# Delta rule into MLP on one core: another order in the last round, on SyncE's queue, and for the norm weight

## The chip, the core and the metric

The kernel runs on one core of a Trainium2 chip. The metric is the device time of one launch in microseconds (us), lower is better; the median of several runs is given with their lowest and highest.

## What is computed

The input x has 128 sequences of 32 tokens with 512 features (4096 tokens), the context 257 positions per sequence. Three residual steps follow each other; the change lies in the second.

```
x = x + cross_attention(layernorm(x), context)
x = x + delta_block(layernorm(x))
x = x + hadamard_quantised_ffn(layernorm(x))           # inner width 2048

delta_block(x):                                        # 32 heads of 16 features
    h = rms(x) * attn_norm
    q, k, v = silu(silu(causal_conv4(h @ W.T)))        # one W and one conv each
    q, k = q / |q|, k / |k| (per head);  beta = sigmoid(h @ Wbeta.T)
    per token, per head:  S -= beta * (S k - v) k^T;  o = S q
    x = x + (rms(o) * out_norm) @ Wout.T
    h2 = rms(x) * mlp_norm
    return x + (silu(h2 @ Wgate.T) * (h2 @ Wup.T)) @ Wdown.T      # inner width 1408
```

All of it is in fp32, apart from the last step's quantised matrices. The norm weights are not ones: they are drawn around one.

## The kernel before

Four stages follow each other: cross_attention, delta_products, delta_out_mlp, and hadamard_ffn, with a Substitution (the solution of the delta rule's triangular systems, on VectorE) that is run in slices beside the second and third. Between stages data goes through DRAM buffers: kd (normal k and q of the last group), ld and pd (products of k with k and of q with k), vd (v with beta), rq (one over the length of q), ud (solutions).

**delta_products** works in 8 rounds of 512 tokens (groups). A round has 12 steps, each the 128 output channels of one of q, k, v: `channels` runs four matmuls of 128x512 (L520), ScalarE scales the last tap (L525), VectorE adds three taps (L527), `activated` applies silu twice (L534, L535). Order of a round: k and q alternating for four chunks, then v four times. Beside the steps run the products of the group before (`multiply`, L455, from masked copies kqm that SyncE loads, L550), the sums of squares per head on TensorE (`Group.add`, L579 to L581), their square roots (`lengths`, L588), the transposition of lengths and beta to tokens (`by_tokens`, L594 to L604), the reciprocal of q's lengths and its store to rq (L606 to L609), and `put_v`: transposes of v (L618), scaling (L621), beta put beside it (L624, GpSimd), store to vd (L625). In each round put_v handles the v of the group before; in the last round there is no later round, so its own four put_v follow the last step. In the last round k and q are stored to kd by SyncE (L666) rather than masked at once, since the products of that group ("late products") are made in the next stage.

**delta_out_mlp** works in 16 blocks of 256 tokens, two tiles of 128 each. `back(b)` prepares block b: per tile it loads u (L743) and copies it to um (GpSimd, L750), loads pe in eight pieces (L757), multiplies (L764), loads xs (L771) and r (L773), and writes oT, the product of both (L777); then squares and a mean over features (L780 to L783), the matmul with Wout (L797), residual and norm (L800 to L811), and the transposition (L97) into hT, copied by ScalarE (L812). `mlp(b)` runs 11 steps of gate and up matmuls (L823, L826) with silu and product (L828, L829), then the down-projection (L834). `late_products` makes 16 products of the last group; each needs eight loads into the single buffer km (L856) and one of k (L858). `mixed` interleaves such generators by their costs: it always advances the one with the smallest share of its total done. Within a block mlp, back of the next block, two late products and the substitution are mixed.

The first block has no block before it. Ahead of it stand the loads of the weights (load_rows, L103: wo, then the norm weight mnw at L874, wg and wu in two halves of columns, the causal mask cm at L879), the first four units of `back(0)` and one late product, the loading of the out-norm weight onw and its multiplication onto wo (scaled_rows, L403 and L406, on VectorE), the load of wd, 16 multiplications of mnw onto wg and wu (L888, on ScalarE), and the rest of back(0) with three late products. The program is written as one sequence; a scheduler then sets each engine's own order, an engine runs its order strictly, and so does each engine's queue of DMA issues. SyncE issues nearly all loads, GpSimd most stores. A DMA issue on SyncE also waits for the transfer that it issued eight before. Tile pools hold buffers; a stage's pools lie where those of the stage before lay, so a first load into a tile waits for the last reader of what lay there.

Of the kernel before, what the change touches and what calls it, by code (L numbers as in the profile page):

```python
# [100 lines left out]
def load_rows(nc, dst, src):  # L101

    nc.sync.dma_start(dst, src.rearrange("(c p) n -> p c n", p=P))  # L103
# [361 lines left out]
def delta_products(  # L465
# [11 lines left out]
    stack, (xp, wp1, hp, wk1, wp, st, wk, wp2, wk2, wp3, wk3, psn, psp, ps, psg) = pools(  # L477
        tc, ("b_x", 3), ("b_w1", 1), ("b_hn", 2), ("b_h", 2), ("b_w", 1), ("b_st", 2), ("b_k", 2),
        ("b_w2", 1), ("b_v", 2), ("b_m", 4), ("b_g", 6), ("b_pn", 1, PSUM), ("b_pp", 3, PSUM),
        ("b_ps", 2, PSUM), ("b_pg", 2, PSUM),  # L480
    )
    with stack:
        w, cw = {}, {}
        for n, src, p in (("k", wkT, wp1), ("q", wqT, wp1), ("v", wvT, wp2)):
            w[n] = p.tile([P, DC, D], FP, name=f"w{n}")
            load_rows(nc, w[n], src)
# [11 lines left out]
        kqm = [wp3.tile([P, HH, 2, KT], FP, name=f"kqm{i}", bufs=1) for i in range(3)]  # L498
# [67 lines left out]
        class Group:  # L566
# [16 lines left out]
            def lengths(self):  # L583

                f = self.factors = wk.tile([3 * H, SG], FP, name="f", bufs=1)
                nc.scalar.activation(f[H : 2 * H], self.sums[H : 2 * H], AF.Tanh, scale=0.5)
                for r in (slice(0, H), slice(2 * H, 3 * H)):
                    nc.scalar.activation(f[r], self.sums[r], AF.Sqrt)  # L588

            def by_tokens(self):  # L590
# [13 lines left out]
                nc.vector.tensor_mul(self.beta, self.beta, n2)  # L604
                q = f[2 * H :]
# [32 lines left out]
        def a_round(gi, old, hT, made):  # L638
# [3 lines left out]
            if gi + 1 < NG:  # L642
                hT_next = wk1.tile([P, DC, SG], FP, name="hT")
                made.append(hT_next)
            for j, (n, ec) in enumerate(todo):
                if n == "v":
                    dst = new.v[ec] = wk2.tile([P, SG], FP, name="v2", bufs=4)
                else:
                    if n == "k":
                        kq[ec] = wp3.tile([P, 2, SG], FP, name="kq")  # L650
                    dst = kq[ec][:, "kq".index(n)]
# [9 lines left out]
                if n == "q":  # L661
                    if gi < NG - 1:
                        pieces.extend((gi, ec, half, kq[ec]) for half in range(SG // KT))
                        hold()
                    else:
                        nc.sync.dma_start(kd[:, ec], kq[ec])  # L666
                if 3 <= j <= 9 and j % 2:
                    new.add(kq[(j - 3) // 2], hT, (j - 3) // 2)
                if j in loads and gi + 1 < NG:
# [7 lines left out]
                if j >= 8 and gi + 1 < NG:  # L677
# [4 lines left out]
            if gi + 1 == NG:  # L682
                for ec in range(DC):
                    new.put_v(ec)

# [4 lines left out]
        for gi in range(NG):  # L690
            made = []
            mixed((len(todo), a_round(gi, old, hT, made)), *beside(gi))
            old, hT = made[0], made[-1]
# [3 lines left out]
def delta_out_mlp(  # L697
# [14 lines left out]
    with stack:  # L712
# [6 lines left out]
        cm = lp.tile([P, T], FP, name="cm")  # L719
        wo = wp.tile([P, DC, D], FP, name="wo")  # L720
        wg = wp.tile([P, DC, FF], FP, name="wg")
        wu = wp.tile([P, DC, FF], FP, name="wu")
        wd = wp.tile([P, FC, D], FP, name="wd")
# [9 lines left out]
        def back(b):  # L733
# [76 lines left out]
            for i in range(NTL):  # L810
                nc.vector.tensor_scalar_mul(ys[i], ys[i], r[:, i : i + 1])  # L811
                nc.scalar.copy(hT[:, :, i * P : (i + 1) * P], g.transposed(ps, ys[i], g.ident))  # L812
# [60 lines left out]
        nw = st.tile([P, DC], FP, name="mnw", bufs=1)  # L873
        nc.sync.dma_start(nw, norm_w.rearrange("(c p) -> p c", p=P))  # L874

        for cols in (slice(0, 6 * P), slice(6 * P, FF)):
            for t, src in ((wg, wgT), (wu, wuT)):
                load_rows(nc, t[:, :, cols], src[:, cols])
        nc.sync.dma_start(cm, causal)  # L879
        mark = []  # L880
        first, late = back(0), late_products()
        mixed((4.0, part(first, 4.0)), (1.0, part(late, 1.0)))
        scaled_rows(nc, st, "onw", onorm_w, [wo])
        load_rows(nc, wd, wdT)
        for cols in (slice(0, 6 * P), slice(6 * P, FF)):
            for t in (wg, wu):
                for dc in range(DC):
                    nc.scalar.mul(t[:, dc, cols], t[:, dc, cols], nw[:, dc : dc + 1])  # L888
        mixed((12.0, first), (3.0, part(late, 3.0)))
# [306 lines left out]
```

## Time and profile before

| | us |
|---|---|
| median of 3 runs | 3079.94 |
| lowest, highest | 3078.09, 3083.41 |
| the profiled execution | 3080.81 |
| its span | 3079.0 |
| TensorE (PE) busy | 2934.2 (95%) |
| VectorE (DVE) busy | 2059.5 (67%) |
| ScalarE (ACT) busy | 1090.1 (35%) |
| GpSimd (POOL) busy | 706.0 (23%) |

About 1.8 us of the execution lie around the span. The mean clock that TensorE was granted is 0.984 of full speed. A page of the profile shows busy time in 40 slices of 77 us, the costliest groups of instructions by line, and a chain of waits, followed back from the end; SPq, DVEq and so on are the engines' sequencers, an L number is a line of the kernel. Matmuls of fp32 appear as two records each, and records of one engine may overlap slightly.

The stages on the time axis: cross_attention to about 706 us, delta_products to 1229 us (its last round begins at 1176.20), first gate matmul of the MLP at 1288.49 us, last blocks done at about 2415 us, then the Hadamard FFN.

### The profile page before, as it was taken

Reading aid. Unit: us, or ns where it says so; the run is one execution under the profiler, and the core shown is the slowest. Engines: PE = TensorE matmul, PEld = TensorE weight load, DVE = VectorE, ACT = ScalarE, POOL = GpSimd, SP = SyncE. Lnnn points to the kernel's source line nnn. Section 1 sums busy time; section 2 is a strip of 40 time slices with the busy share of each in tenths; the row PEclk is TensorE's granted clock in tenths of the full one; section 3 lists DMA queues with packets and bytes.
Section 4 is the critical chain, followed back from the end, with each engine's and each line's share of the span. In section 5 each row is a group of like instructions: output and inputs, shape, how many; then the busy total and the mean of one; then the engine's idle time right before and its main releaser. Section 6 shows DMA issues by size and latency. Waiting matters only on the chain.

```text
span 3079.0 us, 42048 instructions
## 1 busy us (share of the span) xinstructions
PE 2934.2 (95%) x15558; PEld 1683.7 (55%) x15558; DVE 2059.5 (67%) x3432; ACT 1090.1 (35%) x1812; POOL 706.0 (23%) x995
## 2 busy tenths in 40 slices
PE   8999999999999999599999999999999899999997
PEld 3444344443333333367676666667777566666664
DVE  2353434326699797378778787878422599999996
ACT  1111111215656666312221112111111366666665
POOL 1121212112686675321212111011000010000001
PEclk9999999999999999799999999999999999999998
DMA  9797989863554544641423323131411111111110
GB/s 332 265 311 269 307 306 310 274 213 98 166 148 131 173 129 132 198 126 59 128 74 106 97 66 112 48 101 50 139 42 42 55 42 42 42 42 35 39 31 21
DMA packets 258236, 408.09 MB, mean 133 GB/s; under 512 B 68336, under 2 KB 170864, under 8 KB 254576
## 3 DMA queue, kind: packets, MB, share of 16 engines
q1 hardware_dynamic: 223856, 305.21, 31.7%
q0 software_dynamic: 34176, 100.19, 9.5%
q8 instruction: 124, 2.03, 0.3%
q14 instruction: 80, 0.66, 0.1%
HBM read 288.36 MB, written 93.85 MB: 124 GB/s over the span
## 4 chain that ended last, share of the span: by engine, by line
PE 41%; DVE 17%; ACT 5%; issue 3%; DMA 2%; SPq 0%; POOL 0%; DVEq 0%; POOLq 0%; ACTq 0%
PE pm L834 9%; PE pm L823 9%; PE pm L826 9%; PE pp L520 5%; PE ps L797 3%; DVE mb L127 3%; ACT t L956 3%; DVE mb L126 2%; DVE mx L1016 2%; DVE m L126 2%; PE pg L455 2%; PE ps L764 2%; DVE m L1002 1%; DVE m L127 1%; DVE W L442 1%
## 5 line engine op out<-in xcount | busy, mean ns | idle before, releaser
L823 PE MATMUL pm<-hT,wg 128*128 128x256 f32 x1408 | 342.1, 386 | 0.7 <-ACT hT L812 0.7
L826 PE MATMUL pm<-hT,wu 128*128 128x256 f32 x1408 | 333.3, 379 | 0.0
L436 DVE TENSOR_TENSOR pr<-L,W 128x1984 f32<-128x1984 f32 (+30 forms) x248 | 312.1, 1258 | 24.6 <-DMA L<-ld 20.6
L442 DVE TENSOR_TENSOR W<-W,pr 128x1984 f32<-128x1984 f32 (+30 forms) x248 | 309.0, 1246 | 3.2
L834 PE MATMUL pm<-wd,mT 128*128 128x512 f32 x704 | 307.2, 592 | 0.0
L823 PEld LDWEIGHTS pm<-hT,wg 128*128 128x128 f32 x1408 | 262.2, 191 | 57.5 <-issue 16.2
L826 PEld LDWEIGHTS pm<-hT,wu 128*128 128x128 f32 x1408 | 267.2, 190 | 36.2
L834 PEld LDWEIGHTS pm<-wd,mT 128*128 128x128 f32 x704 | 132.6, 190 | 160.8 <-issue 160.7
L828 ACT ACTIVATE sg<-pm 128x256 f32<-128x256 f32 x176 | 67.4, 383 | 350.1 <-PE pm L823 340.1
L829 DVE TENSOR_TENSOR mT<-pm,sg 128x256 f32<-128x256 f32 x176 | 73.8, 419 | 164.1 <-PE pm L826 150.0
L1042 POOL TENSOR_TENSOR xo<-xo,xt 128x512 f32<-128x512 f32 x32 | 42.7, 1336 | 581.6 <-ACT xo L1041 581.6
L996 PE MATMUL ps<-wq,qT 128*128 128x512 bf16 x512 | 133.1, 383 | 28.9 <-DVE m L1002 17.3
L956 ACT ACTIVATE t<-ps,magic,qs 128x512 f32<-128x512 f32 x160 | 117.6, 777 | 96.5 <-DVE qs L951 96.4
L461 POOL TENSOR_TENSOR kk<-kk,cm 128x256 f32<-128x256 f32 x128 | 135.5, 1058 | 2.1
L999 PE MATMUL ps<-wq,qT 128*128 128x512 bf16 x512 | 132.4, 381 | 2.2 <-DVE m L1002 2.2
L458 POOL DMA_DIRECT2D ld<-kk x128 | 92.2, 720 | 147.4 <-ACT kk L457 140.4
L346 PE MATMUL ps<-hT,wq 128*128 128x512 f32 x256 | 118.6, 623 | 7.2 <-ACT hT L339 7.2
L939 PE MATMUL ps<-hd,mT 128*128 128x128 f32 x1024 | 121.5, 277 | 0.0
L455 PE MATMUL pg<-kqm,kq 128*32 128x512 f32 x896 | 118.8, 601 | 2.1 <-DMA kqm<-kq 1.5
L302 PE MATMUL ps<-wo,aoT 128*128 128x512 f32 x256 | 118.8, 608 | 1.5 <-ACT aoT L295 1.5
L520 PE MATMUL pp<-hT,wk 128*128 128x512 f32 x256 | 118.6, 604 | 0.3 <-DVE acc L527 0.3
L1039 PE MATMUL ps<-wq,q2T 128*128 128x512 bf16 x512 | 117.2, 383 | 0.9 <-ACT q2T L1033 0.9
(217 smaller groups left out, 5220.6 us busy)
## 6 DMA issues: line engine op xcount, KB each, us to landing
kall<-in_ctxT_dram SPq DMA_DIRECT2D x32, 2056.0 KB
cx<-in_ctx_dram SPq DMA_DIRECT2D x32, 2048.0 KB
x<-xo POOLq DMA_DIRECT2D x64, 256.0 KB, 3.4
xt<-x SPq DMA_DIRECT2D x64, 256.0 KB
ld<-kk POOLq DMA_DIRECT2D x128, 128.0 KB, 2.5
pd<-kk POOLq DMA_DIRECT2D x128, 128.0 KB, 2.3
L<-ld SPq DMA_DIRECT2D x8, 2048.0 KB
pe<-pd SPq DMA_DIRECT2D x256, 64.0 KB
```

Source lines behind the costliest of these rows:

```text
L126: nc.vector.tensor_add(o[:, :, 0, :], i[:, :, 0, :], i[:, :, 1, :])
L436: nc.vector.tensor_mul(pr[:, 0:n], bc(L[:, s, :, s + 1 : T].rearrange("p h t -> p t h"), HD), w[:, s].unsqueeze(1).to_broadcast([P, n, H4, ...
L442: nc.vector.tensor_sub(w[:, s + 1 :], w[:, s + 1 :], pr[:, 0:n])
L455: nc.tensor.matmul(pg[js], k[:, js], m[:, :, :, js], start=True, stop=True)
L461: nc.gpsimd.tensor_mul(kk[:, 1], kk[:, 1], cm.unsqueeze(1).to_broadcast([P, HH, T]))
L520: nc.tensor.matmul(pp.rearrange("p b t -> p (b t)"), w[n][:, dc, ec * P : (ec + 1) * P], hT[:, dc, :], start=dc == 0, stop=dc == DC - 1,)
L823: nc.tensor.matmul(pg, wg[:, dc, fs], hT[:, dc, :], start=dc == 0, stop=dc == DC - 1)
L826: nc.tensor.matmul(pu, wu[:, dc, fs], hT[:, dc, :], start=dc == 0, stop=dc == DC - 1)
L834: nc.tensor.matmul(pd, mT[:, fc, i * P : (i + 1) * P], wd[:, fc, :], start=fc == 0, stop=fc == FC - 1,)
L956: nc.scalar.activation(t, pr, AF.Identity, bias=magic, scale=qs)
L996: nc.tensor.matmul(pg, qT[:, dc, :], wg[:, dc, ks], start=dc == 0, stop=dc == DC - 1)
L999: nc.tensor.matmul(pu, qT[:, dc, :], wu[:, dc, ks], start=dc == 0, stop=dc == DC - 1)
```

## The change

It has four parts.

1. In delta_products the weights wq and wv swap pools and the order of loading: wv is now loaded early with wk, wq where wv was. The pairs kq get a pool of their own, kqm too.
2. The last round is a function of its own, `last_round`: the order of its steps is k four times, v four times, q four times. Two products run per step. The sums of squares are made separately for k (with beta) and for q (`add_one`); lengths and by_tokens for k and beta come in the v steps; each q step stores its pair to kd from ScalarE's queue and puts one chunk of the group's own v away; q's lengths and their reciprocal (`put_q`, split off by_tokens) come last.
3. In delta_out_mlp SyncE's order changes: wo, wg, wu, wg, wu first, then all loads of back(0) for both tiles (four units of it), then cm, onw and mnw, then wd, then the late products' loads; all four of the early late products now come after the first four units of back(0). The tile of wd is allocated ahead of the other weights.
4. The MLP's norm weight is no longer multiplied onto wg and wu. Instead the transposed norm output is multiplied by it on its way into hT: per tile four pieces of 128x128, two on ScalarE and two on VectorE.

```diff
--- before.py
+++ after.py
@@ -100,7 +100,7 @@
 
 def load_rows(nc, dst, src):
 
-    nc.sync.dma_start(dst, src.rearrange("(c p) n -> p c n", p=P))
+    return nc.sync.dma_start(dst, src.rearrange("(c p) n -> p c n", p=P))
 
 
 def mixed(*steps):
@@ -474,14 +474,14 @@
     tc, nc = g.tc, g.nc
     KT = 256
 
-    stack, (xp, wp1, hp, wk1, wp, st, wk, wp2, wk2, wp3, wk3, psn, psp, ps, psg) = pools(
+    stack, (xp, wp1, hp, wk1, wp, st, wk, wp2, kqp, wk2, wp3, wk3, psn, psp, ps, psg) = pools(
         tc, ("b_x", 3), ("b_w1", 1), ("b_hn", 2), ("b_h", 2), ("b_w", 1), ("b_st", 2), ("b_k", 2),
-        ("b_w2", 1), ("b_v", 2), ("b_m", 4), ("b_g", 6), ("b_pn", 1, PSUM), ("b_pp", 3, PSUM),
+        ("b_w2", 1), ("b_kq", 4), ("b_v", 2), ("b_m", 1), ("b_g", 6), ("b_pn", 1, PSUM), ("b_pp", 3, PSUM),
         ("b_ps", 2, PSUM), ("b_pg", 2, PSUM),
     )
     with stack:
         w, cw = {}, {}
-        for n, src, p in (("k", wkT, wp1), ("q", wqT, wp1), ("v", wvT, wp2)):
+        for n, src, p in (("k", wkT, wp1), ("q", wqT, wp2), ("v", wvT, wp1)):
             w[n] = p.tile([P, DC, D], FP, name=f"w{n}")
             load_rows(nc, w[n], src)
         w["b"] = wp.tile([P, DC, H], FP, name="wb")
@@ -495,7 +495,7 @@
         nc.sync.dma_start(cm, causal)
         scaled_rows(nc, wp, "nw", norm_w, [w["k"], w["q"], w["v"], w["b"]])
 
-        kqm = [wp3.tile([P, HH, 2, KT], FP, name=f"kqm{i}", bufs=1) for i in range(3)]
+        kqm = [wp3.tile([P, HH, 2, KT], FP, name=f"kqm{i}") for i in range(3)]
         blank = [t[:, h] for t in kqm for h in range(HH)]
         mv, rs = stats
 
@@ -580,12 +580,24 @@
                 nc.tensor.matmul(self.sums[H : 2 * H], w["b"][:, ec, :], hT[:, ec, :], **at)
                 nc.tensor.matmul(self.sums[2 * H :], hs[:, ec, :], sq[:, 1], **at)
 
-            def lengths(self):
-
-                f = self.factors = wk.tile([3 * H, SG], FP, name="f", bufs=1)
-                nc.scalar.activation(f[H : 2 * H], self.sums[H : 2 * H], AF.Tanh, scale=0.5)
-                for r in (slice(0, H), slice(2 * H, 3 * H)):
-                    nc.scalar.activation(f[r], self.sums[r], AF.Sqrt)
+            def add_one(self, kq, hT, ec, of):
+
+                sq = wk.tile([P, 2, SG], FP, name="sq")
+                nc.scalar.activation(sq[:, 0], kq[:, "kq".index(of)], AF.Square)
+                at = dict(start=ec == 0, stop=ec == DC - 1)
+                rows = slice(0, H) if of == "k" else slice(2 * H, 3 * H)
+                nc.tensor.matmul(self.sums[rows], hs[:, ec, :], sq[:, 0], **at)
+                if of == "k":
+                    nc.tensor.matmul(self.sums[H : 2 * H], w["b"][:, ec, :], hT[:, ec, :], **at)
+
+            def lengths(self, of="kq"):
+
+                if "k" in of:
+                    f = self.factors = wk.tile([3 * H, SG], FP, name="f", bufs=1)
+                    nc.scalar.activation(f[H : 2 * H], self.sums[H : 2 * H], AF.Tanh, scale=0.5)
+                for n, r in (("k", slice(0, H)), ("q", slice(2 * H, 3 * H))):
+                    if n in of:
+                        nc.scalar.activation(self.factors[r], self.sums[r], AF.Sqrt)
 
             def by_tokens(self):
                 f = self.factors
@@ -602,6 +614,9 @@
                 nc.vector.tensor_mul(n2, self.n, self.n)
                 nc.vector.reciprocal(n2, n2)
                 nc.vector.tensor_mul(self.beta, self.beta, n2)
+
+            def put_q(self):
+                f = self.factors
                 q = f[2 * H :]
                 nc.vector.tensor_scalar_max(q, q, 1e-12)
                 nc.vector.reciprocal(q, q)
@@ -639,15 +654,14 @@
             new = Group(gi)
             made.append(new)
             xt, kq = [], {}
-            if gi + 1 < NG:
-                hT_next = wk1.tile([P, DC, SG], FP, name="hT")
-                made.append(hT_next)
+            hT_next = wk1.tile([P, DC, SG], FP, name="hT")
+            made.append(hT_next)
             for j, (n, ec) in enumerate(todo):
                 if n == "v":
                     dst = new.v[ec] = wk2.tile([P, SG], FP, name="v2", bufs=4)
                 else:
                     if n == "k":
-                        kq[ec] = wp3.tile([P, 2, SG], FP, name="kq")
+                        kq[ec] = kqp.tile([P, 2, SG], FP, name="kq")
                     dst = kq[ec][:, "kq".index(n)]
                 acc, last = channels(hT, n, ec)
                 with tc.issue_after(last):
@@ -659,14 +673,11 @@
                         multiply()
                 activated(acc, dst)
                 if n == "q":
-                    if gi < NG - 1:
-                        pieces.extend((gi, ec, half, kq[ec]) for half in range(SG // KT))
-                        hold()
-                    else:
-                        nc.sync.dma_start(kd[:, ec], kq[ec])
+                    pieces.extend((gi, ec, half, kq[ec]) for half in range(SG // KT))
+                    hold()
                 if 3 <= j <= 9 and j % 2:
                     new.add(kq[(j - 3) // 2], hT, (j - 3) // 2)
-                if j in loads and gi + 1 < NG:
+                if j in loads:
                     xt.append(load((gi + 1) * GT + len(xt)))
                 if j == 9:
                     new.lengths()
@@ -674,23 +685,57 @@
                         g.factors(*(t[:, EARLY:] for t in stats))
                 if j == 11:
                     new.by_tokens()
-                if j >= 8 and gi + 1 < NG:
+                    new.put_q()
+                if j >= 8:
                     normed((gi + 1) * GT + j - 8, xt[j - 8], hT_next)
                 if old and j < DC:
                     old.put_v(j)
                 yield 1
-            if gi + 1 == NG:
-                for ec in range(DC):
+
+        def last_round(gi, old, hT):
+
+
+            new = Group(gi)
+            kq = []
+            for j, (n, ec) in enumerate((n, ec) for n in "kvq" for ec in range(DC)):
+                if n == "k":
+                    kq.append(kqp.tile([P, 2, SG], FP, name="kq"))
+                if n == "v":
+                    dst = new.v[ec] = wk2.tile([P, SG], FP, name="v2", bufs=4)
+                else:
+                    dst = kq[ec][:, "kq".index(n)]
+                acc, _ = channels(hT, n, ec)
+                for _ in range(2):
+                    if count["done"] < per * len(held):
+                        multiply()
+                activated(acc, dst)
+                if n == "q":
+                    nc.scalar.dma_start(kd[:, ec], kq[ec])
                     new.put_v(ec)
+                if j < DC:
+                    old.put_v(j)
+                if 1 <= j <= DC:
+                    new.add_one(kq[j - 1], hT, j - 1, "k")
+                elif j == DC + 1:
+                    new.lengths("k")
+                elif j == DC + 2:
+                    new.by_tokens()
+                elif n == "q" and ec:
+                    new.add_one(kq[ec - 1], hT, ec - 1, "q")
+                yield 1
+            new.add_one(kq[DC - 1], hT, DC - 1, "q")
+            new.lengths("q")
+            new.put_q()
 
         hT = wk1.tile([P, DC, SG], FP, name="hT")
         for i in range(GT):
             normed(i, load(i), hT)
         old = None
-        for gi in range(NG):
+        for gi in range(NG - 1):
             made = []
             mixed((len(todo), a_round(gi, old, hT, made)), *beside(gi))
-            old, hT = made[0], made[-1]
+            old, hT = made
+        mixed((len(todo), last_round(NG - 1, old, hT)), *beside(NG - 1))
         assert count["done"] == per * len(pieces)
 
 
@@ -717,10 +762,10 @@
         for t in (*um, *pe, km):
             nc.gpsimd.memset(t, 0.0)
         cm = lp.tile([P, T], FP, name="cm")
+        wd = wp.tile([P, FC, D], FP, name="wd")
         wo = wp.tile([P, DC, D], FP, name="wo")
         wg = wp.tile([P, DC, FF], FP, name="wg")
         wu = wp.tile([P, DC, FF], FP, name="wu")
-        wd = wp.tile([P, FC, D], FP, name="wd")
         inv_d = st.tile([P, 1], FP, name="inv_d", bufs=1)
         nc.vector.memset(inv_d, 1.0 / D)
         turn = {"pe": 0, "um": 0}
@@ -809,7 +854,11 @@
             hT = wk2.tile([P, DC, TB], FP, name="hT")
             for i in range(NTL):
                 nc.vector.tensor_scalar_mul(ys[i], ys[i], r[:, i : i + 1])
-                nc.scalar.copy(hT[:, :, i * P : (i + 1) * P], g.transposed(ps, ys[i], g.ident))
+                pt = g.transposed(ps, ys[i], g.ident)
+                for dc in range(DC):
+                    (nc.vector.tensor_scalar_mul if dc % 2 else nc.scalar.mul)(
+                        hT[:, dc, i * P : (i + 1) * P], pt[:, dc, :], nw[:, dc : dc + 1]
+                    )
                 yield 2
             ready[b] = hT, xs
 
@@ -870,23 +919,21 @@
                     k = masked(*todo[n + 1])
 
         load_rows(nc, wo, woT)
-        nw = st.tile([P, DC], FP, name="mnw", bufs=1)
-        nc.sync.dma_start(nw, norm_w.rearrange("(c p) -> p c", p=P))
 
         for cols in (slice(0, 6 * P), slice(6 * P, FF)):
             for t, src in ((wg, wgT), (wu, wuT)):
-                load_rows(nc, t[:, :, cols], src[:, cols])
-        nc.sync.dma_start(cm, causal)
+                weights = load_rows(nc, t[:, :, cols], src[:, cols])
         mark = []
         first, late = back(0), late_products()
-        mixed((4.0, part(first, 4.0)), (1.0, part(late, 1.0)))
-        scaled_rows(nc, st, "onw", onorm_w, [wo])
+        nw = st.tile([P, DC], FP, name="mnw", bufs=1)
+        with tc.issue_after(weights.ins):
+            for _ in range(4):
+                next(first)
+            nc.sync.dma_start(cm, causal)
+            scaled_rows(nc, st, "onw", onorm_w, [wo])
+            nc.sync.dma_start(nw, norm_w.rearrange("(c p) -> p c", p=P))
         load_rows(nc, wd, wdT)
-        for cols in (slice(0, 6 * P), slice(6 * P, FF)):
-            for t in (wg, wu):
-                for dc in range(DC):
-                    nc.scalar.mul(t[:, dc, cols], t[:, dc, cols], nw[:, dc : dc + 1])
-        mixed((12.0, first), (3.0, part(late, 3.0)))
+        mixed((8.0, first), (4.0, part(late, 4.0)))
         for b in range(NBL):
             mixed(
                 (3.5 * FC + 9.5 * NTL, mlp(b)),
```

## The prediction

> **What bounds the kernel now.** I read the page's slices first, then busy time by stretches, the timelines of PE, SP and ACT in the gap that shows there, and the chain of waits through it.
>
> ```profile
> PE   8999999999999999599999999999999899999997
> PEclk9999999999999999799999999999999999999998
> ```
>
> TensorE (PE) sets the pace nearly everywhere; the one hole before the last stage is slice 16, where its clock drops too. That is the passage from the delta rule's last round (ends 1229.2 us) to the MLP's first matmul (L823, 1288.5). By stretches (columns: length, busy PE, PEld, DVE, ACT, POOL, PEclk, DMA share, GB/s):
>
> ```profile
> 1230.00:1240.00 10.00, 1.38 (x10) 0.93 (x9) 9.92 (x14) 9.35 (x14) 2.58 (x6) 0.67 0.93 332
> 1240.00:1250.00 10.00, 1.47 (x7) 0.98 (x5) 0.19 (x2) 7.97 (x11) 3.08 (x5) 0.50 1.12 275
> 1250.00:1260.00 10.00, 3.64 (x64) 2.80 (x64) 2.47 (x5) 0.00 (x0) 6.21 (x9) 0.50 1.06 302
> 1260.00:1270.00 10.00, 4.73 (x43) 2.61 (x44) 2.23 (x7) 1.22 (x2) 2.43 (x5) 0.50 0.58 143
> 1804.50:1878.00 73.50, 73.07 (x392) 52.07 (x391) 63.60 (x96) 14.78 (x27) 7.76 (x9) 1.00 0.17 52
> ```
>
> The last row is one MLP block of 256 tokens: PE 73.07 of 73.50, DVE 63.60. So a block has nothing to give and little room; the passage has some 45 us of idle PE. What ends late there, from the chain of waits:
>
> ```profile
> 1230.76 3.35 DVE f L607
> 1234.39 2.22 POOL rq L609 x4
> ...
> 1240.26 5.53 DMA vd<-vt
> 1245.86 16.93 DMA wd<-in_WdownT_dram
> ...
> 1268.33 6.57 DMA r<-rq
> 1274.95 0.04 issue
> 1275.00 0.70 DVE oT L777
> ...
> 1279.67 1.04 PE pm L455 x8
> ```
>
> The MLP weights queue on SP behind the norm weight, issued only at 1229.31; the last down-projection load (wd) takes 16.93 us, the second tile's loads stand behind it, and oT is whole at 1275.7. After that comes a second chain, the "late products": L455 needs km, a single buffer that eight SP loads refill only when the product before has read it:
>
> ```profile
> 1279.60 1.06 PE L455 MATMUL pm<-km,k 128*32 128x512 f32 x8
> 1283.24 0.66 PE L97 MATMUL ps<-ident,y 128*128 128x128 f32 x4 [2.58 <-DVE y L811]
> 1284.10 0.66 PE L97 MATMUL ps<-ident,y 128*128 128x128 f32 x4 [0.21 <-DVE y L811]
> 1286.63 1.94 PE L455 MATMUL pm<-km,k 128*32 128x512 f32 x8 [1.87 <-issue]
> 1288.49 3.47 PE L823 MATMUL pm<-hT,wg 128*128 128x256 f32 x8
> ```
>
> From the second product's end (1280.66) to the third's start 5.97 us pass; to the fourth's (1288.57 to 1295.94) 7.37. In before the third product's trip lies beside the norm and the transposes L97, so it costs about 2.
>
> **What the Trainium skill says.** "DMA: Bandwidth & Descriptors", Anatomy of one DMA: some 2.0 us fixed per transfer plus bytes over 436 GB/s. The trace agrees on the fixed part: the third product's k load is issued by 1284.76, the product starts 1.9 later. For wd (2816 KB) the page gives 8.6; the trace shows 16.93, since the queue held other weights. "Trainium Kernel Development and Optimization", Key Constraints: queues share the same DMA engines, another issuer saves issue time only; so kd stores on ACT's queue buy no bandwidth. No trace of before has an ACT DMA issue; SP's take 0.3 to 0.5. "TensorE: Matmul & The Clock Gate", Part 1: an idle PE falls to half clock until about 3.4 us of work. The trace agrees: 64 L764 records take 3.64 at clock 0.50, 1.96 at full. "ScalarE: Activation LUTs", What ACT_TABLE_LOAD costs: 0.19 plus 0.83 ns per element, 0.09 for a per-partition scale, overlapping by 0.09: about 0.29 per scaled 128x128 piece (estimate); its 0.61 for the 128x512 copy is 0.59 in the trace (L812).
>
> **The change, part by part.**
>
> *wq and wv swap places* (round 0). wv is loaded with wk early, wq late. In before wv's scaling ran on DVE from 708.53 for 1.68 us; wq, scaled in that slot, is needed by the second channel at 710.28. Its first two pieces are done by 709.5, the last by 710.2. Cost 0 to 2; I take 0.3. Behind it on PE is the whole round.
>
> *Last round in order k, v, q.* PE's work stays: 12 channels of 3.5, products 4.8, old and own put_v, sums. What moves ahead of the last channel is the beta transpose (L594, 0.46) and three own put_v (about 0.6 each); two of q's sums move behind it. So the last q matmul ends at 1229.2+1.8+0.5+0.3=1231.8 (1230 to 1233). Then in a row: put_v 0.6, scaling from PSUM 0.64, three taps 1.92, two silus 1.26, square 0.63, sum 0.6, table load and sqrt 1.88, maximum 0.42, reciprocal 3.34, four rq issues 2.22, and about 1.6 of hand-overs (8 by 0.2): 15.1, so POOL is free at 1246.9 and its um copies (0.80 each) let the first L764 start at 1247.5, where before it was 1255.66 behind vt's 10.03 us wait for vd. Put_v for v no longer waits there.
>
> *SP's order.* wo and wg issue after the last kqm load (about 1193.5), wu about 1200; the second wu waits for the first kd store (about 1228), as SP waits for the transfer eight before. Behind it stand u and all pe loads: they issue to 1244, xs and r to 1245; in before 1241.9. That wait is covered, as the um copies come at 1247; uncovered it would cost 2 to 4. L764 cold 3.64, oT at 1252. The second r (single buffer) goes out at 1253.9 once that is read; landing 4.3 (1295.22 to 1299.52 in a quiet stretch) to 6.57: second oT done at 1259.7, sixteen earlier than 1275.7. wd goes out behind it at 1256 and lands about 1266 (8.6 by the page; bounds 1264 to 1273); its first reader is long after.
>
> *What is late next.* onw lands behind r, so wo's four scalings (0.48 each) stand between: 1.7. L797, 16 records, begins cold: 7.0 warm, 8.7 so. To 1269. From L797's end to L97's end before took 5.1 (1279.66 to 1284.76): 1273.5 (1271 to 1277). The order of PE in the changed build has three late products behind L97 and ahead of the first MLP matmul, where before only the last stood there with its trip half hidden. So: first product to 1274.5, trip 6.0 to 7.0 and product 1.06 to 1281.9, again to 1288.6 to 1289: first MLP matmul 1288.5 (1286 to 1292), before 1288.49. Of the sixteen nothing is left. Ahead of it lie now all 64 L764 records of the next block (2.16 saved), behind it the fourth product waits 2.5 instead of 1.23: together -0.9, bounds -4 and +4.
>
> *Norm weight on hT.* The 16 scalings L888 (3.40+0.94+2.57+2.97+2.97=12.85 us of ACT, 1232.6 to 1248) go; in before they ran beside the wait for vd and wd, so nothing by themselves. Per block two copies of 0.59 become four ACT and four DVE pieces. DVE's row nearest, n<-ps 128x128, took 0.29: +1.1 a block, 17.6 in all, on an engine with 9.9 idle of 73.5. It counts only where PE waits: between the second L97 and the matmul that needs the last DVE piece the build leaves PE 3.4 us of other work (32 matmuls of L764 1.96, one each of the gate, up and late product 1.4), and that piece stands behind about 4 us of DVE work (taps of the substitution, statistics, centring, butterflies), of which three matmuls more hide the rest. 0 to 0.3 a block: I take +1 (0 to +5). If that cover went, the 4 would show in full, 60 in all. mnw, late on SP, lands long before its first use.
>
> Sum: 3080.81 (the profiled run, span 3079.0) +0.3-0.9+1 = 3081.2, some 0.9 above the median of 3079.94 as that run is: 3080 in its terms.
>
> **Rivals.** *The gain stands*: if the km trips overlap the norm (L97 nearer 1268, scaling of wo and the cold clock costing nothing) only one trip of 6 stands in the path, as before: -16+6 = -10, 3070 (3064 to 3074). For it: the chain of before ends in wd and r, both freed, and the ACT table stays on sqrt in the tail. Against: PE's order, and one km buffer.
>
> *DVE holds hT back (slower)*: at a block's start the last hT piece waits behind a pair of L436/L442, up to 2.1 us each in their widest form. From the point where DVE's queue ahead of it exceeds about 5 us, PE stops: 0.7 a block by 15 is +10.5, 3090 (3086 to 3096). For it: PE has no slack there, and now DVE as well as ACT must be on time. Against: DVE's share drops with the narrow forms; before, PE waited for hT 0.7 us in the whole stage.
>
> *It doesn't do what it says*: u and pe behind the kd stores land only after 1250; the first L764 is back at 1252, all is 4 later: 3084.
>
> **How the numbers follow.** Gain eaten by the trips 0.44 (3080, own range 3073 to 3086), gain stands 0.33, DVE holds hT 0.19, no early start 0.04. A change under 0.2% (6.2 us) can't be told from none. Faster: 0.33 and 0.03 of the first's tail; slower: 0.19 and 0.02. The range leaves out the outer part of both rivals: 3066 to 3090.
>
> **What would show it.** Right: L764 first near 1247.5; second oT near 1260; three L455 groups 6 to 7 us apart between L97 and the first gate matmul, that at 1286 to 1292; blocks of 73.5. Wrong: the first gate matmul before 1282 (gain stands); waits of PE for hT from DVE of over 0.5 a block (slower); a first wq matmul after 711 (swap).

## The result, and the profile after

The changed kernel took 3086.91 us (median of 9 runs, 3083.59 to 3092.6), the kernel before beside it 3080.24 (9 runs); the ratio is 1.0017 with a 95% interval of 1.0005 to 1.0029. So it is slower, by about 5 us. That lies under the 0.2% that the forecast set as the bound of no change, though the interval reaches over it. The forecast was 3080, 3066 to 3090, with "no change" the likeliest.

The profiled executions say the same: spans 3083.6 and 3079.0, +4.6. Both profiles begin delta_products at 706.8 us, so their times can be compared directly here. In the later runs that start lies between 698.6 and 708.5 although nothing ahead of it was changed. For that reason lengths of stages are compared below, not spans.

The PE and PEclk slices of the page have the same digits as before; the hole in slice 16 is there still. By stretches, with the columns of before:

```profile
1230.00:1240.00 10.00, 7.15 (x22) 2.52 (x20) 5.56 (x9) 4.70 (x9) 3.22 (x5) 1.00 0.93 254
1240.00:1250.00 10.00, 1.92 (x2) 0.18 (x2) 3.76 (x2) 2.84 (x4) 3.72 (x5) 0.53 0.79 184
1250.00:1260.00 10.00, 6.38 (x116) 5.58 (x120) 2.53 (x5) 0.63 (x1) 2.00 (x5) 0.67 0.84 191
1260.00:1270.00 10.00, 8.50 (x39) 3.72 (x30) 3.95 (x10) 1.62 (x4) 1.26 (x1) 0.94 0.86 289
1270.00:1280.00 10.00, 2.96 (x17) 1.04 (x16) 3.20 (x8) 3.06 (x8) 4.07 (x6) 0.74 0.35 89
1280.00:1290.00 10.00, 4.30 (x72) 2.76 (x72) 0.00 (x0) 0.59 (x1) 2.04 (x3) 0.67 0.36 105
1804.50:1878.00 73.50, 73.47 (x394) 52.39 (x393) 64.98 (x98) 15.85 (x31) 7.64 (x10) 1.00 0.16 49
```

The last two of the 10 us stretches were, in the kernel before:

```profile
1270.00:1280.00 10.00, 9.48 (x54) 3.97 (x57) 3.16 (x7) 2.89 (x5) 1.09 (x2) 0.95 0.43 126
1280.00:1290.00 10.00, 5.35 (x28) 2.31 (x21) 1.98 (x4) 4.01 (x9) 5.29 (x8) 0.73 0.25 74
```

PE's idle time has moved: from 1230 to 1270 PE is busy for 24.0 us instead of 11.2, from 1270 to 1290 for 7.3 instead of 14.8, and VectorE and ScalarE do nearly nothing from 1280 to 1290. The MLP block is as full as it was (73.47 of 73.50), with VectorE up by 1.4. Two views, of TensorE and of the chain, show what the idle stretch is:

```profile
1262.58 2.22 PE L842 MATMUL ps<-wo,oT 128*128 128x512 f32 x4 [1.50 <-DVE wo L406]
...
1272.95 1.09 PE L97 MATMUL ps<-ident,y 128*128 128x128 f32 x8 [2.78 <-DVE y L856]
1274.49 1.70 PE L455 MATMUL pm<-km,k 128*32 128x512 f32 x8 [0.45 <-DMA k<-kd]
1281.96 1.94 PE L455 MATMUL pm<-km,k 128*32 128x512 f32 x8 [5.76 <-DMA pe<-pd]
1283.63 2.62 PE L809 MATMUL ps<-pe,um 128*32 128x128 f32 x64
1291.02 1.94 PE L455 MATMUL pm<-km,k 128*32 128x512 f32 x8 [4.76 <-DMA k<-kd]
1292.89 3.15 PE L872 MATMUL pm<-hT,wg 128*128 128x256 f32 x8
```

```profile
1249.49 5.18 DMA r<-rq
...
1254.76 0.70 DVE oT L822
...
1259.44 12.57 DMA wd<-in_WdownT_dram
1272.03 0.30 SPq L905
1272.38 1.88 DMA k<-kd
...
1274.49 1.72 PE pm L455 x8
```

The second oT is done at 1262.0 and the transposes end at 1274.0, where before these were 1275.7 and 1284.8. Then three late products come one by one, each behind a refilling of km (the second one's wait is put down to a load of pe, issued 0.47 us after the load of k that it needs), and the first gate matmul stands at 1292.9 where it stood at 1288.5. In the chain wd still takes 12.57 us, but it lands at 1272.0, before the transposes begin, and the load of k behind it lands as they end; only 0.45 us of waiting show on PE.

The stages of both kernels and of all eleven experiments are in this table, read from their traces (us). "Round" is the last round of delta_products from its first to its last channel matmul (L520); the four columns after it count from its end: first matmul of the first tile (L764 of before, L809 of after), end of the second oT, end of L97, first gate matmul. "MLP" is from there to the end of the last down-projection, "whole" from the first matmul of delta_products to the end of the kernel. Ratios are those of the timed runs. Lengths are differences of rounded times, so right to about 0.1.

| kernel | round | first tile | 2nd oT | L97 | gate | MLP | whole | ratio to before (95%) |
|---|---|---|---|---|---|---|---|---|
| before | 53.1 | 26.4 | 46.4 | 55.5 | 59.2 | 1126.6 | 2372.2 | 1 |
| after | 60.8 | 16.2 | 27.5 | 39.5 | 58.4 | 1126.1 | 2376.8 | 1.0017 (1.0005 to 1.0029) |
| e1 after, no early late products | 61.9 | 16.5 | 28.6 | 43.3 | 43.7 | 1132.7 | 2373.4 | 0.9996 (0.9985 to 1.0008) |
| e2 before, no early late products | 53.1 | 26.9 | 42.2 | 52.6 | 53.5 | 1128.8 | 2371.5 | 0.9992 (0.9980 to 1.0003) |
| e3 before, new round | 56.1 | 6.4 | 52.0 | 63.9 | 65.7 | 1124.5 | 2380.2 | 1.0030 (1.0021 to 1.0040) |
| e4 after, old round | 53.1 | 21.5 | 35.1 | 49.7 | 67.6 | 1126.1 | 2378.4 | 1.0030 (1.0020 to 1.0039) |
| e5 after, 4 vt buffers | 56.1 | 16.2 | 27.8 | 43.2 | 60.9 | 1126.4 | 2376.8 | 1.0004 (0.9996 to 1.0012) |
| e6 before, norm weight on hT | 53.1 | 26.5 | 46.0 | 55.6 | 58.8 | 1128.5 | 2372.6 | 1.0004 (0.9996 to 1.0011) |
| e7 as e4, no early late products | 53.1 | 21.2 | 34.1 | 48.1 | 48.5 | 1132.6 | 2368.3 | 0.9992 (0.9982 to 1.0002) |
| e8 as e7, 4 vt buffers | 53.1 | 18.9 | 31.8 | 45.5 | 46.0 | 1130.9 | 2361.8 | 0.9978 (0.9969 to 0.9987) |
| e9 as e8, wo scaled early | 53.1 | 19.3 | 33.0 | 41.1 | 41.6 | 1132.4 | 2359.1 | 0.9958 (0.9946 to 0.9969) |
| e10 as e1, 4 vt buffers | 56.1 | 16.2 | 27.5 | 40.8 | 41.2 | 1132.4 | 2362.1 | 0.9976 (0.9965 to 0.9987) |
| e11 as e10, wo scaled early | 56.1 | 16.6 | 31.6 | 39.5 | 40.0 | 1132.7 | 2365.2 | 0.9948 (0.9936 to 0.9960) |

So of the +4.6 the last round gives +7.7, the passage behind it -0.8, the MLP -0.5; what is left, -2.5 ahead of that round and +0.7 in the last stage, is of the size that those stretches vary by with unchanged code (466.4 to 470.5 from the start of delta_products to its last round in the five kernels that keep the old delta_products whole, 663.9 to 666.1 in the last stage of all). Each kernel has one trace, and in the passage too a length varies: the changed kernel, e1 and e5 have the same code from the second oT to the end of L97 and took 12.0, 14.6 and 15.4 there. Differences of 3 us in one column behind the round therefore prove nothing alone. The round itself is steady: 53.1 in seven kernels, 56.1 in four.

### The profile page after: what moved, and what is told of

It is laid out like the page before. It is cut to its first block, busy times and chain, and to the rows that moved or that the text cites. A ratio compares the mean times of both kernels' runs of the same rounds, so it can differ in the third digit from the quotient of the medians.

```text
span 3083.6 us, 42052 instructions
## 1 busy us (share of the span) xinstructions
PE 2944.1 (95%) x15496; PEld 1684.2 (55%) x15558; DVE 2073.4 (67%) x3496; ACT 1080.0 (35%) x1830; POOL 690.1 (22%) x995
## 3 DMA queue, kind: packets, MB, share of 16 engines
q1 hardware_dynamic: 223280, 303.12, 31.6%
## 4 chain that ended last, share of the span: by engine, by line
PE 45%; DVE 14%; ACT 5%; issue 2%; DMA 1%; POOL 1%; SPq 1%; DVEq 0%; POOLq 0%; ACTq 0%
PE pm L872 10%; PE pm L883 10%; PE pm L875 10%; PE pp L520 5%; PE ps L842 3%; DVE mb L127 3%; ACT t L1003 3%; DVE mb L126 2%; DVE mx L1063 2%; PE ps L809 2%; DVE m L126 2%; PE pg L455 2%; DVE m L1049 1%; DVE m L127 1%; PE ps L97 1%
## 5 line engine op out<-in xcount | busy, mean ns | idle before, releaser
L872 PE MATMUL pm<-hT,wg 128*128 128x256 f32 x1408 | 348.4, 387 | 0.5 <-ACT hT L859 0.5
L1043 PE MATMUL ps<-wq,qT 128*128 128x512 bf16 x509 | 132.5, 382 | 30.8 <-DVE m L1049 17.3
L1046 PE MATMUL ps<-wq,qT 128*128 128x512 bf16 x484 | 126.2, 381 | 2.2 <-DVE m L1049 2.2
L461 POOL TENSOR_TENSOR kk<-kk,cm 128x256 f32<-128x256 f32 x128 | 126.2, 986 | 2.1
L520 PE MATMUL pp<-hT,wk 128*128 128x512 f32 x256 | 119.1, 606 | 0.4 <-DVE acc L527 0.4
L520 PE MATMUL pp<-hT,wv 128*128 128x512 f32 x256 | 118.0, 605 | 0.0
```

Of the source, the lines that this page charges most:

```text
L461: nc.gpsimd.tensor_mul(kk[:, 1], kk[:, 1], cm.unsqueeze(1).to_broadcast([P, HH, T]))
L520: nc.tensor.matmul(pp.rearrange("p b t -> p (b t)"), w[n][:, dc, ec * P : (ec + 1) * P], hT[:, dc, :], start=dc == 0, stop=dc == DC - 1,)
L872: nc.tensor.matmul(pg, wg[:, dc, fs], hT[:, dc, :], start=dc == 0, stop=dc == DC - 1)
L1043: nc.tensor.matmul(pg, qT[:, dc, :], wg[:, dc, ks], start=dc == 0, stop=dc == DC - 1)
L1046: nc.tensor.matmul(pu, qT[:, dc, :], wu[:, dc, ks], start=dc == 0, stop=dc == DC - 1)
```

## The experiments

**The km trips.** Theory: the gain at the second oT was given back to the three late products ahead of the first block. Rival: those trips only fill a wait that is there anyway. The edit takes them out of that stretch; they then start with block 0, so nothing is left out.

```diff
-        mixed((8.0, first), (4.0, part(late, 4.0)))
+        mixed((8.0, first))
```

e1, the changed kernel with it:

> The changed kernel, with none of the late products (L455 from km) in the stretch before the first block; they start with block 0, two per block, as the others do. Theory (the gain was given back to km trips that stand in a row between the transposes L97 and the first gate matmul): in the changed kernel PE stood idle there for 0.45+5.76+4.76 us and 1.20 more before the fourth product, 12.2 in all; about 1 of it comes back as the wait for the first hT. First gate matmul at 1275 to 1277 us instead of 1292.9, the time 10 to 12 us below the changed kernel (about 3076, ratio to the kernel before about 0.9985). Rival (the new last round and the pieces of hT cost the time, and km trips only fill a wait that is there anyway): the first gate matmul stays after 1287 and the time within 3 us of the changed kernel.

```profile
1280.67 1.97 PE L97 MATMUL ps<-ident,y 128*128 128x128 f32 x8 [2.79 <-DVE y L856]
1283.10 3.78 PE L872 MATMUL pm<-hT,wg 128*128 128x256 f32 x8 [0.46 <-ACT hT L859]
```

The gate matmul follows L97 at once; counted from the round's end it comes 14.7 us earlier (43.7 against 58.4), though L97 itself came 3.8 later in this trace. 6.6 come back in the MLP, where the three products (1.06 each) and the next block's L809 (2.16) now stand; the expectation had left this return out. At 1283.1 the gate matmul is later than the 1275 to 1277 expected, and by the ratios the run is 6.5 us under the changed kernel, less than the 10 to 12 expected; besides the return, the trace shows the later L97. The rival fails: the gate matmul did not stay.

e2, the same in the kernel before (there the early products stood in two calls of `mixed`, both lose them):

> The kernel before, with the same edit: no late product ahead of the first block. Theory: the third product's trip (1.87 idle) and the fourth's (1.23) go, 3 us. Besides, the second tile's u, pe, xs and r no longer stand on SP behind eight km loads of which the last waited for wd (1262.8); r can go out some 5 us earlier, so 3 to 9 us below the kernel before, first gate matmul 1280 to 1285. Rival (the gap of the kernel before is wd's landing alone): second oT still near 1275, at most 3 us below.

Gate 53.5 after the round's end, 5.7 earlier, the second oT 4.2 earlier; the MLP takes 2.2 more. The ratio 0.9992 cannot be told from 1, and its 2.5 us are under the 3 to 9 expected. The rival, in which the second oT stays, fails by the stage lengths; the time alone proves nothing. In the kernel before the trips cost little, as the prediction read them.

**Each half alone.** e3 is the kernel before with the new delta_products, e4 the changed kernel with the old one; whole functions are exchanged.

> The kernel before with only the delta_products of the change (wq and wv swapped, last round in order k, v, q, kd stores from ScalarE), its MLP stage as before. Theory: the last matmul of the round ends at 1232 (no weight loads beside the vd stores, so no wait of PE for sq as in the changed kernel, 2.98 us), first L764 about 1249 to 1252 rather than 1255.7, but wd, queued behind the weights on SP, still lands after 1260 and the second r behind it: time within 4 us of the kernel before. Rival (the new round itself costs 5 us, as its last matmul ends 5.3 later in the changed kernel): 4 to 8 us above the kernel before, with the round ending at 1234 or later.

The round takes 56.1, 3.0 more than the old order, close to what the prediction gave it (2.6); PE waits for nothing in it, so this is work that now stands ahead of the last channel. The first tile's L809 comes only 6.4 after its end (17 to 20 expected). But the kernel is 0.3% slower, 9 us: the rival's size and more, though not in its place, the round. My theory's 4 us fail. The chain of this run says why:

```profile
1227.31 0.70 DVE vt L636
...
1229.28 6.95 DMA vd<-vt
...
1236.57 0.37 SPq L103
...
1238.95 18.64 DMA wu<-in_WupT_dram
```

In this build SyncE issues the weights at 1236.6, once the last vd store has landed, and with them wd and the second tile's pe and r follow late (second oT 52.0 after the round). The new round alone moves the weights later; the change of SyncE's order alone has the opposite trouble:

> The changed kernel with the delta_products of before (q and k alternating, v last, kd stored from SyncE): only the MLP stage's order on SyncE and the norm weight on hT are changed. Theory: the round ends near 1229 to 1232, the first tile's L809 waits again for the last vt and vd on VectorE and GpSimd, 1253 to 1256; the second oT about 3 to 5 later than the changed kernel's 1262.0, the three km trips unchanged behind it: first gate matmul 1293 to 1298, time 0 to 5 us above the changed kernel. Rival (the new round is a net loss of 3 to 5 us): time 3 to 5 us below the changed kernel.

First tile at 21.5 (L764 in this kernel), second oT at 35.1, then 17.9 us from L97 to the gate matmul (18.9 in the changed kernel): gate at 67.6, ratio 1.0030. Each half alone costs 0.3%, both together 0.17%, so their costs do not add; that one half is slower than both is not shown, as the intervals overlap. The rival for e4, that the new round is a net loss, fails.

**The round's extra 4.7 us.** e3 gives 56.1 for the new order, the changed kernel needs 60.8. VectorE in that round, changed kernel:

```profile
1200.46 0.69 DVE L636 TENSOR_TENSOR vt<-ps,n 128x512 f32<-128x512 f32 x1 [6.43 <-DMA vd<-vt]
1201.07 2.21 DVE L527 SCALAR_TENSOR_TENSOR acc<-pp,cwk,acc 128x496 f32<-128x496 f32 x3
```

The fourth put_v of the group before waits 6.43 us for a buffer of vt; behind it on VectorE stand the taps of k, behind those ScalarE's silus and squares, and PE waits 2.98 for a square. SyncE had issued wo and the first wg, 2.5 MB, at 1191.4 and 1191.8. e5 gives vt two buffers more in the changed kernel:

```diff
-                vt = wk2.tile([P, GT, HH, HD + 1], FP, name="vt")
+                vt = wk2.tile([P, GT, HH, HD + 1], FP, name="vt", bufs=4)
```

> The changed kernel with four buffers instead of two for vt (the scaled v on its way to vd). Theory (the last round is 7.7 us longer than before, 60.8 against 53.1, because the weight loads that now start at 1191 hold up the vd stores, vt waits 6.43 us for its buffer on VectorE, and with it the taps of k, the squares, and PE 2.98 us and some more in the next v step): the round takes 56 to 57 us as in the run with only the new round (56.2), 4 to 5 less than the changed kernel; the rest unchanged, so time 3 to 5 us below it. Rival (PE is held in that round by the weight loads' own traffic against the kqm loads, or by ScalarE's order): the round stays at 60 or more.

The round takes 56.1, 4.7 less, so the rival (60 or more) fails. The ratio falls from 1.0017 to 1.0004, but these intervals overlap, and in the trace L97 came 3.7 later after the round's end, so its whole is no shorter (2376.8). Part of that is PE's clock in the passage: twelve records of L842 took 5.40 in the changed kernel's trace, where the granted clock was 1.00, and 6.23 in e5's, where it was 0.87. A clearer case for the time is e10 below, which is e1 with this edit alone: the round falls from 61.9 to 56.1, the ratio from 0.9996 to 0.9976, 6 us.

That the stores of vd are slow beside the weight loads can be read from their landings in the first half of the round. In e3, where no weights load there, the stores issued from 1186 to 1196 took 2.8 to 3.6 us to land. In the changed kernel the one issued at 1192.1, behind wo and wg, took 8.27. In e5, where wo and wg are issued at 1186.4 and 1186.8, those issued from 1186 to 1195 took 8.3 to 9.0. So four buffers do not make the stores faster, but the fourth put_v no longer waits for them (e5):

```profile
1192.08 0.69 DVE L636 TENSOR_TENSOR vt<-ps,n 128x512 f32<-128x512 f32 x1 [3.00 <-PE ps L633]
```

No run held the loads back in the changed kernel with all else as it was.

**The norm weight.** e6 is the kernel before with L888 taken out and the eight pieces per block put in.

> The kernel before with only the norm weight moved: no scaling of wg and wu, four pieces of hT on ScalarE and four on VectorE per block. Theory: nothing in the passage (the 16 scalings lay beside the wait for wd), blocks longer by 0 to 0.3 us as PE's work is cut into smaller groups of one shape, 0 to 4 us in all: from the first gate matmul to the last down-projection 1127 to 1131 us, before 1126.6. Rival (VectorE's half of hT holds PE at each block): 1133 us or more, with waits of PE for hT from VectorE. Second rival (12.85 us of ScalarE work were in the way of the last v): the first gate matmul comes over 3 us earlier after the round's end than the 59.2 us of before.

MLP 1128.5, +1.9 (e3, with the old code there, has 1124.5, so a part of this is scatter between traces); gate matmul at 58.8 after the round (59.2). All that PE waits for in this run from 1304 to 2415, and in the changed kernel to 2425 (waits: total, times, longest):

```profile
PE pm L827 <- ACT hT L814: 0.5, 1, 0.5
```

```profile
PE ps L986 <- ACT zT L1017: 0.7, 1, 0.7
PE pm L872 <- ACT hT L859: 0.5, 1, 0.5
```

VectorE's half never holds PE up. Both rivals of this experiment fail: neither the blocks nor the passage change by 3 us.

**Toward a faster version.** e7 is e4 without early late products, e8 has four vt buffers besides.

> The MLP stage of the change (order on SyncE, norm weight on hT) with the delta_products of before, and no late product ahead of the first block. Theory: round 53.1 us, first gate matmul 50 us after its end (67.6 in the run with the km trips, less their 17.9 and some cold clock), MLP stage 1132 us with the products moved into it: from the start of delta_products to the end 2366 to 2369 us, before 2372.2, after 2376.8; time 3 to 6 us below before, ratio 0.998 to 0.999. Rival (what is saved ahead of the first block comes back inside the blocks): MLP stage over 1134, ratio 1.000.

Gate 19.1 earlier than in e4, MLP 6.5 longer, ratio from 1.0030 to 0.9992: the second time that the trips are taken out, with the other round, and the step is 11.7 us by the ratios. The rival's 1134 for the MLP did not come. Against the kernel before, the interval still holds 1.

> As the run with the old round and no early late products, and vt with four buffers: the last four put_v of the round no longer wait for the stores to vd. Theory: PE's wait for vt in the tail (7.42 us) and GpSimd's later um copies go, first L764 some 5 to 8 us earlier, and with the second r that waits for oT the whole tail: gate matmul 43 to 46 us after the round's end; 5 to 8 us below the run without, ratio to before about 0.996. Rival (the pe loads or the second r on SyncE set the tail): first L764 earlier but the second oT and the gate matmul within 2 us of the run without.

First tile 2.3 earlier, gate 2.5, less than the 5 to 8 expected, and within the 3 us that prove nothing alone. PE's wait for vt after the round stays (7.43 us in this trace), so it was not the vd store that held those two put_v but VectorE's own queue; in the trace of before the reciprocal and the last taps keep VectorE busy from 1230.8 to 1238.8. What the buffers removed are the waits of the last two put_v for vd, 6.99 and 1.74 us on VectorE in e7 (10.03 and 1.27 in the kernel before). The ratio is 0.9978, with an interval that overlaps that of e7.

What stands in the way then is wo: PE waits 2.82 for its scaling in e8, and 3.55 in e10. In e9 and e11 the scaling goes ahead of the first block's tiles:

```diff
+            scaled_rows(nc, st, "onw", onorm_w, [wo])
             for _ in range(4):
                 next(first)
             nc.sync.dma_start(cm, causal)
-            scaled_rows(nc, st, "onw", onorm_w, [wo])
```

> As the run with the old round, four vt buffers and no early late products, and the out-norm weight is loaded and multiplied onto wo ahead of the first block's tiles instead of behind the second oT. Theory (the scaling of wo and the cold clock behind its wait were 2.82 us of PE idle and some 2 to 4 of half clock): L797 starts at or before the second oT, transposes L97 end 3 to 5 us earlier after the round's end than 45.5, gate matmul at 41 to 43; time 3 to 5 us below the run without, ratio to before 0.996 to 0.997. Rival (L97 is set by the second oT, with the scaling beside it): gate matmul 45 to 46 as it was.

L97 comes at 41.1 instead of 45.5, the ratio is 0.9958. The theory holds, the rival does not: the second oT came 1.2 later and L97 4.4 earlier, since six records of the matmul with wo now run before that oT is done.

> The changed kernel, all four parts, with no early late products and four vt buffers: against the run that differs in the round alone (old round, ratio 0.9978) it tells what the new order of the round is worth once the weight loads no longer hold it up. Theory: the new round is 3.1 longer (56.2 against 53.1), first L809 16.2 after its end against 18.9, second oT 27.8 against 31.8: a wash, within 2 us of that run, ratio 0.997 to 0.999. Rival (the new order is a gain that the other faults hid): 4 us or more below it, ratio under 0.9965.

0.9976 against 0.9978 of e8: a wash, as the theory said. The round is 3.0 longer and the tail 4.3 to 4.8 shorter.

> As the run before this one, with the scaling of wo ahead of the first block's tiles too. Theory: as with the old round 3 to 5 us less, ratio 0.996 to 0.9975. Rival: on VectorE the scaling stands behind the reciprocal of q's lengths and ahead of the first oT; if it delays that oT by its 1.7 us, nothing is gained.

All four parts, with the three edits, give 3065.45 us (5 runs), ratio 0.9948, 16 us under the kernel before and the lowest median here. This is 8.6 us less than e10, more than the 3 to 5 expected. The rival's delay of the first oT was 0.4, not 1.7; the second oT came 4.1 later, behind six records of L842, and L97 1.3 earlier. PE's waits in the passage of e11, 1226 to 1270 us (total, times, longest):

```profile
PE ps L809 <- DMA xs<-x: 7.8, 1, 7.8
PE pn L589 <- ACT sq L586: 4.3, 2, 3.5
PE ps L97 <- DVE y L856: 2.8, 1, 2.8
PE pm L828 <- DVE sq L827: 2.4, 1, 2.4
PE pm L872 <- ACT hT L859: 0.5, 1, 0.5
```

No line of km, wo or wd is left; what remains is the chain of q's lengths and the norm itself. The first line names xs, but L809 started 0.05 us after the end of GpSimd's first copy of u to um (1243.37), which stood behind the stores of q's reciprocal; in the changed kernel the same wait is 7.41 and put down to that copy. The profiled execution of e11 does not show the gain in full (whole 2365.2, e9's 2359.1), as its first round took longer (65.9 us against 63.3 in e9); the gain rests on the timed runs, and most of the 8.6 us is not explained by the trace. Whether old or new round is better in that company is open: e9 and e11 overlap in their intervals.

## Why the prediction was right, and where it was off

The likeliest case and its mechanism were right: the gain at the second oT was eaten by the trips of km (e1 and e7), and the time moved by 0.17%, under the 0.2% that was called no change. It was near the edge, and luck helped. In the forecast's terms 1.0017 is 3085.2, with 3086 as the end of the likeliest case's own range. The first gate matmul came 4.4 later than predicted, and that is a sum of errors that partly cancel: the round began 2.5 earlier and took 5.2 more than predicted, the way to the second oT 0.4 less, from there to L97 1.8 less, from L97 to the gate 3.9 more. Taken step by step:

- *Swap of wq and wv.* First wq matmul 710.35 (710.28 before): nothing, 0.3 predicted.
- *Last round.* This step failed in its size. It said "PE's work stays" and put the last q matmul at 1231.8; it ended at 1234.5. The new order cost 3.0 (e3), close to the 2.6 worked out; what was missing is the 4.7 of e5: the weight loads, which the same change brings forward to 1191, slow the stores of vd, and put_v of the group before has only two buffers. Each part was costed alone; this term belongs to two of them together. That the round began 2.5 earlier in this trace hides part of it in the absolute time.
- *Tail.* From the round's end to the first tile 16.2 (15.7 predicted), to the second oT 27.5 (27.9): right.
- *SyncE's order.* The last pe of the first tile was issued at 1248.6, not by 1244: the second pe waited for the last kd store, which took 5.46 us to land (1245.83), not only for the first ones. The wait for the transfer eight before counts ScalarE's issues with SyncE's in this program, so moving the kd stores to ScalarE's queue did not take them out of SyncE's way. GpSimd's clearing of km waited for that last store too, 7.13 us. The reciprocal ended at 1247.8 beside it, so the cover held, with little left.
- *wd.* Issued at 1259.4, landed about 1272.0, inside the bounds of 1264 to 1273 but later than the 1266 taken; 0.45 of it showed. The formula of the Trainium skill ("DMA: Bandwidth & Descriptors", Anatomy of one DMA) that gave 8.6 is stated there for transfers that GpSimd issues, while SyncE issues wd; the measured 12.57 decides.
- *L97 and trips.* L97 ended at 1274.0 (1273.5 predicted), but this is luck: the terms given from the second oT on, 1.7, 8.7 and 5.1, add to 15.5, the prediction's times leave 13.8 for them, and 12.0 was measured, which made up for most of the late round. From the first product's end to the second's start 5.77, from the second's to the third's 7.12, as predicted (6.0 to 7.0). But the products took 1.70, 1.94 and 1.94 instead of 1.06, at granted clocks of 0.59, 0.50 and 0.50: the mis-sized term of this sum. The prediction's own lines of before have 1.94 for one of them. First gate matmul 1292.9, 0.9 outside the bounds of 1286 to 1292. The fourth product waited 1.20, not 2.5.
- *Norm weight on hT.* +1.9 in the MLP (e6), +1 predicted, bounds 0 to 5.

The rival in which the gain stands needed the trips to overlap the norm; PE's order forbade it, and e1 and e7 show what it would have been worth: 6.5 and 11.7 us. Even so its 10 us under the kernel before would not have come, as e1 stands at 0.9996. The rival in which VectorE holds hT back did not happen: 0.5 us of waits for hT in a stage of 1126. By the stage lengths the slowness came from the round (+7.7, nothing else over +0.7), by a mechanism that no rival named.

## What to carry to other kernels

A wait that is taken away is worth what the next one leaves of it: before moving loads, write down which single buffers are refilled in a row behind the point that is to come earlier, and move those out of the stretch first (here three products: 6 to 12 us). Bulk loads that are brought forward into a busy stage should be checked against that stage's small stores and the number of buffers that wait for them. Costs of the parts of one change need not add (here 0.3% for each half, 0.17% for both), so test them in company too. Where the time alone is too noisy, compare stage lengths in the traces, but find out first how much a stage with the same code varies.

## What the runs showed of the hardware beside this

The stage ahead of delta_products, whose code no run changed, ended between 698.6 and 708.5 us in the profiled executions, so spans alone could not order these kernels. A vd store of 136 KB took 2.8 to 3.6 us to land in e3 with no weights loading and 8.3 to 9.0 in e5 beside them. A scaled 128x128 piece of hT took 0.37 us on ScalarE and 0.34 on VectorE, where the prediction used 0.29 for each. The first eight records of the gate matmul took 1.99 us in e8, at a granted clock of 1.00, and 3.78 in e1, at 0.51, though PE stood idle for 0.46 us before them in both.
